# Mixture of experts behind a recurrent layer: four gathers that add themselves onto a tile, in place of four gathers and four additions

## The chip, the cores and the metric

The kernel runs on one core of one Trainium2 chip. It has TensorE (PE; its weight loads are shown as PEld), VectorE (DVE), ScalarE (ACT), GpSimd (POOL), SyncE (SP), which here only issues DMAs, and 16 DMA engines. The metric is the device time of one execution in microseconds (us); lower is better.

## The reference, cut to what matters

Eight sequences of 512 tokens, 512 wide, go through a layer norm. One branch is a linear attention with decay, gated and normed per head, and projected (s). The other is a mixture of 16 experts of which each token takes four, and a shared expert. The output is x + s * silu(mixture).

```python
routing_weights, selected_experts = jax.lax.top_k(router_probs, K)        # K = 4 of E = 16
routing_weights = routing_weights / routing_weights.sum(axis=-1, keepdims=True)
comb = jnp.sum(jax.nn.one_hot(selected_experts, E) * routing_weights[..., None], axis=1)
for e in range(E):
    mixed = mixed + comb[:, e:e + 1] * _swiglu(flat, Wg[e], Wu[e], Wd[e])
shared = _swiglu(flat, sWg, sWu, sWd)
g = silu(mixed + shared * sigmoid(flat @ shared_gate_w))
...
x = x + s * g
```

All is in float32. A tile is 128 tokens x 512; there are 32.

## The kernel before

**Stages.** First the norms, the routing and the shared expert of all sequences are worked out, beside the attention of sequence 0; the shared part of each tile, already times its gate, goes to DRAM (`sh_d`). The tokens' choices are sorted by expert into blocks of 128 rows. Then, after sequence 1, the blocks go through their experts; each row comes out times its routing weight and goes to DRAM (`y_d`). `place` holds, for each token and each of its four choices, the row of `y_d` that is its own. The last stage is the one that the change touches: the attention of sequences 2 to 7 on PE, and beside it, for all 32 tiles, the mixture and the final x + s * g.

**The mixture of one tile** is a generator, `mixture(b, t)` (L1190), that does one step at each call and yields between:

- step 1: SP loads the shared part from `sh_d` into the tile `m` (L1194, 12 buffers), and for the eight tiles of sequences 0 and 1 the stored projection `s` (L1198); POOL issues the first gather, an indirect DMA of 128 rows of `y_d` into a tile `yg` of its own (L1203, 14 buffers)
- steps 2 to 4: the other three gathers, each into its own `yg`
- step 5: POOL adds the second gather onto the first (L1209); step 6: POOL adds the fourth onto the third (L1212), and DVE adds the first sum onto `m` (L1214)
- step 7: DVE adds the second sum onto `m` (L1217)
- step 8: ACT takes the silu of `m` in place (L1220)
- step 9: for an `s` tile `last` is called; for the others `m` is kept until PE has projected the tile

`last` (L1227) loads x into `xo`, has DVE multiply `m` by `s` or by the projection `pw` in its PSUM bank (L1240), and POOL add it onto `xo` (L1244); SP stores the result (L1245). That last addition is put off by two steps (`late`), except in sequence 7.

**What sets the order.** Each engine has one queue and takes its instructions in order. `behind(engine)` puts an instruction behind the last one traced on that engine. `advance` (L1261) is one step for all open tiles; a new tile is opened each 11/5 steps. The attention's code calls it some 15 times per sequence between its parts, and its own instructions stand in the same queues: the products with the decays, the rotations (`stream_shuffle` L634, L636 to L638), the masked scores (L711) on DVE; the copies of `v` (L587), the silus of q and k (L632), the squares (L744) and the blocks of the state (L694) on ACT. PE multiplies for k and q (L627), v (L583), scores (L685), outputs (L722, L733), the sums of squares (L747) and the projections (L776, in two banks, and L906 in the last sequence).

Of the kernel before, what the change touches and what calls it, by code (L numbers as in the profile page):

```python
# [10 lines left out]
F32 = mybir.dt.float32  # L11
# [5 lines left out]
ALU = mybir.AluOpType  # L17
AX = mybir.AxisListType

P = 128  # L20
B, N, D = 8, 512, 512
# [74 lines left out]
def tile_block(ctx: ExitStack, tc: tile.TileContext, a: dict, out: bass.AP):  # L96
    nc = tc.nc
# [16 lines left out]
    y_d = dram.tile([NB * P, D], F32, name="y_d", tag="y_d")  # L114
# [96 lines left out]
    def behind(engine):  # L211

        last = next(
            (i for i in reversed(nc.cur_bb.bb.instructions) if i.engine == engine), None)
        return tc.issue_after(last) if last else nullcontext()

    POOL, DVE, ACT = (
        mybir.EngineType.Pool, mybir.EngineType.DVE, mybir.EngineType.Activation)
# [948 lines left out]
    with tc.If(count > SURE):  # L1167
# [16 lines left out]
    comb = right.enter_context(  # L1184
        tc.tile_pool(name="comb", bufs=1, side="right", reuse_waits="tile"))

    place = comb.tile([P, TOPK, NT], I32, tag="place", name="place")
    nc.sync.dma_start(place.rearrange("p r t -> p (r t)"), at_d)

    def mixture(b, t):  # L1190

        g = b * NC + t
        m = comb.tile([P, D], F32, tag="m", name=f"m_{b}_{t}", bufs=12)
        nc.sync.dma_start(m, sh_d[b][t * P : (t + 1) * P, :])  # L1194
        s = None
        if b < FIRST:
            s = comb.tile([P, D], F32, tag="s", name=f"s_{b}_{t}", bufs=4)
            nc.sync.dma_start(s, s_d[b][t * P : (t + 1) * P, :])  # L1198
        ys = []
        for r in range(TOPK):  # L1200
            yg = comb.tile([P, D], F32, tag="yg", name=f"yg_{b}_{t}_{r}", bufs=14)
            with behind(POOL):
                nc.gpsimd.indirect_dma_start(  # L1203
                    out=yg, out_offset=None, in_=y_d,
                    in_offset=bass.IndirectOffsetOnAxis(ap=place[:, r, g : g + 1], axis=0))
            ys.append(yg)
            yield
        with behind(POOL):
            nc.gpsimd.tensor_tensor(ys[0], ys[0], ys[1], ALU.add)  # L1209
        yield  # L1210
        with behind(POOL):
            nc.gpsimd.tensor_tensor(ys[2], ys[2], ys[3], ALU.add)  # L1212
        with behind(DVE):
            nc.vector.tensor_tensor(m, m, ys[0], ALU.add)  # L1214
        yield
        with behind(DVE):
            nc.vector.tensor_tensor(m, m, ys[2], ALU.add)  # L1217
        yield
        with behind(ACT):
            nc.scalar.activation(m, m, AF.Silu)  # L1220
        yield
        if s is not None:
            last(b, t, m, s)
        else:
            m_of[b, t] = m

    def last(b, t, m, s):  # L1227
        xo = comb.tile([P, D], F32, tag="xo", name=f"xo_{b}_{t}", bufs=4)
        nc.sync.dma_start(xo, x[b, t * P : (t + 1) * P, :])
        if (b, t) == (B - 1, NC - 1):  # L1230

            for cols in (slice(0, D // 2), slice(D // 2, D)):
                with behind(DVE):
                    nc.vector.tensor_tensor(m[:, cols], m[:, cols], s[:, cols], ALU.mult)
                with behind(DVE):
                    nc.vector.tensor_tensor(xo[:, cols], xo[:, cols], m[:, cols], ALU.add)
                nc.sync.dma_start(out[b, t * P : (t + 1) * P, cols], xo[:, cols])
            return
        with behind(DVE):
            nc.vector.tensor_tensor(m, m, s, ALU.mult)  # L1240

        def add():
            with behind(POOL):
                nc.gpsimd.tensor_tensor(xo, xo, m, ALU.add)  # L1244
            nc.sync.dma_start(out[b, t * P : (t + 1) * P, :], xo)  # L1245

        if b + 1 == B:
            add()
        else:
            late.append((steps[0], add))  # L1250
# [10 lines left out]
    def advance():  # L1261

        if steps[1] < len(tiles) and steps[0] * 5 >= steps[1] * 11:
            active.append(mixture(*tiles[steps[1]]))
            steps[1] += 1
        steps[0] += 1
        while late and late[0][0] + 1 < steps[0]:
            late.pop(0)[1]()
        order = active[:]
        while order:  # L1270
            f = order.pop(0)
            if next(f, f) is f:
                active.remove(f)
            order.reverse()
# [76 lines left out]
```

## Time and profile before

| | us |
|---|---|
| time, median of 3 runs | 1198.29 (1196.13 to 1202.39) |
| the profiled execution's own time | 1193.77 |
| its span in the profile | 1191.9 |
| first gather of the mixture starts | 742.1 |
| POOL: 128 gathers (L1203) busy | 143.0 |
| POOL: one addition of two gathered tiles (L1209), median | 1.284 |
| DVE: one addition onto `m` (L1214, L1217), median | 0.684 |

A row of the page's group list gives an engine, an instruction, what it writes and reads, how often, its busy time and the mean of one, and the idle time just ahead of it with what ended it. A row of the windows gives, for a stretch, its length and the busy time of PE, PEld, DVE, ACT and POOL, then the granted clock of TensorE and the share and rate of DMA. A row of the waits gives who waited for whom, the total, the number of times and the longest. A row of a timeline gives start, duration, engine and line; in square brackets is the idle time before it and what ended it. "issue" is time without a wait that the profile shows; an engine with q (SPq) is its queue.

### The profile page before, as it was taken

To read this page: it belongs to the slowest core of one execution; us is meant where nothing else is said; L and a number is where in the kernel's file an instruction comes from. 1 tells how busy PE (TensorE), PEld (TensorE's weight loads), DVE (VectorE), ACT (ScalarE), POOL (GpSimd) and SP (SyncE) were. 2 spreads that over 40 slices of the span, in tenths; PEclk is the share of its full clock that TensorE was granted. 3 is DMA by queue.
4 is the path that set the end of the run, shared out by engine and by line. 5 is a ranking of instruction groups with operands and counts; after the bars stand their busy time and mean duration, and the time that the engine had idled before them with its cause. 6 is when DMAs were issued, how large, how long until landed. Compare 5 with 4: busy or idle time off the path is not lost. (4 is left out here: it accounts for less than half of the span.)

```text
span 1191.9 us, 21613 instructions
## 1 busy us (share of the span) xinstructions
PE 1145.7 (96%) x7780; PEld 700.9 (59%) x7780; DVE 722.8 (61%) x1557; ACT 459.7 (39%) x934; POOL 452.2 (38%) x432
## 2 busy tenths in 40 slices
PE   7999999989999999999999999999999989999997
PEld 3445554456577777677777775555554645545553
DVE  6356754889124444344444444969979598698684
ACT  4444454144374444444444442251251422422531
POOL 3211203200213333233333331762886848858211
PEclk9998999989999999999999999999999999999999
DMA  9964341191659999899999895931845637534112
GB/s 340 327 236 173 120 168 44 41 377 38 183 160 224 226 227 221 217 232 232 221 227 229 229 226 181 336 120 51 277 133 184 200 95 235 163 115 144 36 35 73
DMA packets 163499, 217.42 MB, mean 182 GB/s; under 512 B 89536, under 2 KB 98880, under 8 KB 161472
## 3 DMA queue, kind: packets, MB, share of 16 engines
q1 hardware_dynamic: 141984, 144.10, 40.5%
q0 software_dynamic: 21120, 70.34, 21.4%
q8 instruction: 65, 1.06, 0.4%
q10 hardware_dynamic: 288, 1.57, 0.4%
q14 instruction: 42, 0.34, 0.1%
HBM read 125.71 MB, written 72.42 MB: 166 GB/s over the span
## 5 line engine op out<-in xcount | busy, mean ns | idle before, releaser
L1103 PE MATMUL pgu<-wexp,xt 128*128 x1088 | 257.8, 380 | 3.2 <-ACT xt L1084 2.7
L1103 PEld LDWEIGHTS pgu<-wexp,xt 128*128 128x128 f32 x1088 | 205.8, 190 | 90.9 <-issue 39.2
L1062 POOL DMA_INDIRECT xg<-xn_d,slot x79 | 75.1, 951 | 243.4 <-DVE y L1133 159.2
L1108 DVE TENSOR_TENSOR slb<-slb,pgu 128x128 f32<-128x128 f32 x136 | 39.2, 288 | 196.7 <-ACT slb L1107 142.0
L1203 POOL DMA_INDIRECT yg<-y_d,place x128 | 143.0, 1117 | 34.6 <-issue 18.6
L1086 ACT COPY xt<-pl 128x512 uint16<-128x512 uint16 x136 | 104.3, 767 | 134.1 <-DMA pl<-xg 77.5
L1124 PE MATMUL py<-wexp,hT 128*128 x272 | 139.3, 594 | 0.1
L583 PE MATMUL pv<-wv,xT 128*128 128x512 f32 x256 | 119.4, 602 | 3.5 <-ACT sh L372 2.3
L627 PE MATMUL pk<-xT,wk 128*128 128x512 f32 x256 | 118.2, 603 | 1.7 <-DVEq L1167 1.7
L627 PE MATMUL pq<-xT,wq 128*128 128x512 f32 x256 | 117.3, 599 | 0.0
L776 PE MATMUL pw<-wo,on 128*128 128x512 f32 x224 | 103.8, 612 | 5.8 <-DVE m L1240 5.2
L1244 POOL TENSOR_TENSOR xo<-xo,m 128x512 f32<-128x512 f32 x31 | 45.1, 1454 | 141.3 <-DVE m L1240 133.4
L1062 POOL DMA_INDIRECT more<-xn_d,slot x57 | 54.0, 947 | 109.9 <-DVE y L1133 109.0
L711 DVE TENSOR_TENSOR sc<-ps,dmask 128x512 f32<-128x512 f32 x128 | 79.5, 680 | 5.6 <-remote 3.8
L627 PEld LDWEIGHTS pq<-xT,wq 128*128 128x128 f32 x256 | 47.8, 193 | 52.8 <-issue 51.3
L627 PEld LDWEIGHTS pk<-xT,wk 128*128 128x128 f32 x256 | 46.1, 190 | 52.0 <-issue 49.6
L1133 DVE TENSOR_SCALAR y<-py,xg 128x512 f32<-128x512 f32 x79 | 59.3, 750 | 28.2 <-PE py L1124 27.7
L776 PEld LDWEIGHTS pw<-wo,on 128*128 128x128 f32 x224 | 42.5, 196 | 56.9 <-issue 47.8
L583 PEld LDWEIGHTS pv<-wv,xT 128*128 128x128 f32 x256 | 45.7, 191 | 49.6 <-issue 43.5
L1107 ACT ACTIVATE slb<-pgu 128x128 f32<-128x128 f32 x136 | 37.8, 278 | 87.5 <-PE pgu L1103 83.1
L694 ACT COPY blocked<-state 32x96 f32<-32x96 f32 x96 | 30.7, 320 | 81.6 <-DVE state L689 68.8
L1133 DVE TENSOR_SCALAR y<-py,more 128x512 f32<-128x512 f32 x57 | 42.7, 750 | 19.7 <-PE py L1124 19.6
(172 smaller groups left out, 1761.5 us busy)
## 6 DMA issues: line engine op xcount, KB each, us to landing
y_d<-y SPq DMA_DIRECT2D x136, 256.0 KB
wexp<-in_experts SPq DMA_DIRECT2D x14, 768.0 KB
sh_d<-sh SPq DMA_DIRECT2D x32, 256.0 KB
m<-sh_d SPq DMA_DIRECT2D x32, 256.0 KB
xo<-in_x SPq DMA_DIRECT2D x32, 256.0 KB
out<-xo SPq DMA_DIRECT2D x31, 256.0 KB
x<-in_x SPq DMA_DIRECT2D x7, 1024.0 KB
xT_d<-xT SPq DMA_DIRECT2D x7, 1024.0 KB
```

What stands on the lines that cost most here:

```text
L583: nc.tensor.matmul(pv, lhsT=xT_of[b][:, k, t * P : (t + 1) * P], rhs=wv[:, k, :], start=(k == 0), stop=(k == KC - 1))
L627: nc.tensor.matmul(ps, lhsT=w[:, k, g * P : (g + 1) * P], rhs=xT_of[b][:, k, :], start=(k == 0), stop=(k == KC - 1))
L711: nc.vector.tensor_tensor(s, pss[j].rearrange("p (c t) -> p c t", t=C), dmask[:, g * HG + j].unsqueeze(1).to_broadcast([P, NC, C]), ALU.mult)
L776: nc.tensor.matmul(pw, lhsT=on_of[b][:, g, t * P : (t + 1) * P], rhs=wo[:, g, :], start=(g == 0), stop=(g == G - 1))
L1062: nc.gpsimd.indirect_dma_start(out=row(i), out_offset=None, in_=xn_d, in_offset=bass.IndirectOffsetOnAxis(ap=slot[:, i : i + 1], axis=0))
L1086: nc.scalar.copy(xt[:, KP:, :].bitcast(U16).rearrange("p k (t h) -> p h k t", h=2), turned(i).rearrange("p (h k) t -> p h k t", h=2))
L1103: nc.tensor.matmul(pg[:, : 2 * F], lhsT=xt[:, k, :], rhs=wflat[:, bass.ds(off + k * 2 * F, 2 * F)], start=(k == 0), stop=(k == KC - 1))
L1108: nc.vector.tensor_tensor(sl, sl, pg[:, F : 2 * F], ALU.mult)
L1124: nc.tensor.matmul(py, lhsT=hT_of.pop(i), rhs=wflat[:, bass.ds(off_of.pop(i) + KC * 2 * F, D)], start=True, stop=True)
L1133: gone.append(nc.vector.tensor_scalar(y, py, row(i).bitcast(F32)[:, bass.ds(at, 1)], None, ALU.mult).ins)
L1203: nc.gpsimd.indirect_dma_start(out=yg, out_offset=None, in_=y_d, in_offset=bass.IndirectOffsetOnAxis(ap=place[:, r, g : g + 1], axis=0))
L1244: nc.gpsimd.tensor_tensor(xo, xo, m, ALU.add)
```

## The change

The four gathers of a tile no longer go to tiles of their own. Each has `compute_op=ALU.add` and `m` as its destination, so that the DMA reads the rows, adds them to what stands in `m` and writes the sums back. The four additions per tile on POOL and DVE are gone, and with them the tiles `yg`. A yield stands between the load of `m` and the first gather, and the steps of the additions are gone, so that a tile now takes seven steps: the load, four gathers, the silu, and the end. As all four gathers of a tile write the same `m`, each waits for the one before to land, and the first for the load of `m`.

```diff
@@ def mixture(b, t) @@
         if b < FIRST:
             s = comb.tile([P, D], F32, tag="s", name=f"s_{b}_{t}", bufs=4)
             nc.sync.dma_start(s, s_d[b][t * P : (t + 1) * P, :])
-        ys = []
+        yield
         for r in range(TOPK):
-            yg = comb.tile([P, D], F32, tag="yg", name=f"yg_{b}_{t}_{r}", bufs=14)
             with behind(POOL):
                 nc.gpsimd.indirect_dma_start(
-                    out=yg, out_offset=None, in_=y_d,
-                    in_offset=bass.IndirectOffsetOnAxis(ap=place[:, r, g : g + 1], axis=0))
-            ys.append(yg)
+                    out=m, out_offset=None, in_=y_d,
+                    in_offset=bass.IndirectOffsetOnAxis(ap=place[:, r, g : g + 1], axis=0),
+                    compute_op=ALU.add)
             yield
-        with behind(POOL):
-            nc.gpsimd.tensor_tensor(ys[0], ys[0], ys[1], ALU.add)
-        yield
-        with behind(POOL):
-            nc.gpsimd.tensor_tensor(ys[2], ys[2], ys[3], ALU.add)
-        with behind(DVE):
-            nc.vector.tensor_tensor(m, m, ys[0], ALU.add)
-        yield
-        with behind(DVE):
-            nc.vector.tensor_tensor(m, m, ys[2], ALU.add)
-        yield
         with behind(ACT):
             nc.scalar.activation(m, m, AF.Silu)
         yield
```

The lines below it move up by twelve: the gather is L1202 in the changed kernel, the silu L1208, the product of `last` L1228, the addition onto `xo` L1232.

## The prediction

> **What bounds the kernel now.** I read the page first (busy shares, slices), then the stage that the change touches by windows, then who waits for whom in it, then the timelines of DVE, PE, POOL and ACT around the two places where PE stands idle.
>
> The mixture runs from the first gather of expert rows at 742.1 us to the end, 449.9 us of the span. TensorE sets the time there as elsewhere:
>
> ```profile
> PE 1145.7 (96%) x7780; PEld 700.9 (59%) x7780; DVE 722.8 (61%) x1557; ACT 459.7 (39%) x934; POOL 452.2 (38%) x432
> 955.00:983.00 28.00, 24.72 (x144) 11.84 (x143) 25.70 (x44) 7.19 (x13) 12.12 (x12) 0.99 0.29 91
> 1036.00:1063.00 27.00, 24.83 (x144) 11.87 (x143) 24.60 (x43) 7.17 (x13) 12.64 (x12) 1.00 0.39 124
> 1120.00:1150.00 30.00, 30.00 (x238) 15.74 (x240) 28.46 (x57) 10.84 (x20) 0.00 (x0) 1.00 0.00 1
> sum 449.00, PE 433.13 PEld 235.60 DVE 352.04 ACT 140.17 POOL 270.36; mean PE 25.48 PEld 13.86 DVE 20.71 ACT 8.25 POOL 15.90
> ```
>
> Columns after the window: its length, then busy us of PE, PEld, DVE, ACT and POOL. PE is idle for 449.0 - 433.1 = 15.9 us of the stage; 5.0 of it lies after 1150, where no mixture runs. So no change to the mixture can win much over 11 us. The two windows with most idle PE, 3.3 and 2.2 us, are ones where DVE is nearly full. From 1120 on DVE is as full and PE loses nothing, so its share alone says little. The first of the two in detail:
>
> ```profile
> 958.43 2.14 DVE L637 TENSOR_TENSOR swk<-swk,sin 128x512 f32<-128x512 f32 x1
> 969.22 0.68 DVE L1214 TENSOR_TENSOR m<-m,yg 128x512 f32<-128x512 f32 x1
> 974.29 0.68 DVE L1217 TENSOR_TENSOR m<-m,yg 128x512 f32<-128x512 f32 x1
> 977.29 1.79 DVE L1214 TENSOR_TENSOR m<-m,yg 128x512 f32<-128x512 f32 x1
> 982.01 0.68 DVE L1240 TENSOR_TENSOR m<-m,pw 128x512 f32<-128x512 f32 x1
> 958.75 1.27 POOL L1209 TENSOR_TENSOR yg<-yg,yg 128x512 f32<-128x512 f32 x1
> 982.74 5.37 PE L776 MATMUL pw<-wo,on 128*128 128x512 f32 x8 [2.90 <-DVE m L1240]
> ```
>
> PE waits at 982.74 for DVE's multiply at 982.01, which frees the bank. DVE has no pause ahead of it from 957.2, and among what it did are the additions that go. L637 took 2.14 us where it takes 0.68 elsewhere: POOL's addition ran beside it. The eight matmuls after the gap took 5.37 us, not 3.6; the granted clock of the window from 983 to 1010 is 0.94.
>
> The other side of the account is POOL's queue and ACT's:
>
> ```profile
> L1203 POOL DMA_INDIRECT yg<-y_d,place x128: 945/1107/1467, 742.1 to 1107.3; - x128
> L1220 ACT ACTIVATE m<-m x32: 621/630/636, 781.4 to 1133.0; 128x512 f32<-128x512 f32 x32
> POOL xo L1244 <- DVE m L1240: 133.4, 18, 38.2
> ACT m L1220 <- DVE m L1217: 20.4, 13, 4.5
> 766.29 1.28 POOL L1212 TENSOR_TENSOR yg<-yg,yg 128x512 f32<-128x512 f32 x1 [1.40 <-DMA yg<-y_d,place]
> ```
>
> A gather keeps POOL 1.107 us. Today POOL never has to wait for one gather before the next, and only five times does it wait for a landing at all: it runs ahead until an xo addition (L1244) holds it for PE's projection. The silus (L1220) stand in ACT's queue between instructions that PE needs.
>
> **The change, part by part.** *Removed from DVE:* 64 additions of 0.60 us start to start, 38 us, and with them the stretching by POOL's additions. In the chain above: 0.6 + 0.6 + 1.7 of additions, 1.5 (L637) and 0.75 (L636 at 961.85, 1.43 us) of stretching, together 5.1 us, more than the 2.9 us that PE waits. So this gap would close, with the slow clock behind it (5.37 - 3.6 = 1.8). With the 2.2 us at 1062 that is 3.3 + 2.2 + 1.8 = 7 us; all idle time would be 11. Where DVE is not late, its additions lie beside matmuls and give nothing.
>
> *Removed from POOL:* 64 additions of 1.28 us, 82 us; no engine waits on POOL's busy time, so this gives only room.
>
> *Moved:* a tile takes seven steps, not nine. Its load of m (SP) now stands one step ahead of its first gather, and the gather waits for it; SP's loads and stores keep their number and order. This load is 256 KB and issued a step (about 5 us) ahead, so I cost it at nothing; where SP sits behind a store that waits for POOL's own xo addition, the price would be one landing, 2 to 3 us, beside the other tiles' gathers. The silu comes two steps earlier in ACT's queue: the last stands behind the ACT instruction that ended at 1126.2. ACT's function loads keep their order. The products of the eight s tiles (L1240) also come two steps earlier on DVE.
>
> *Added:* each gather after a tile's first must wait until the one before it has landed, since both write m. The program makes POOL wait, in order. Behind the waiting gather stand the other tiles' gathers and the xo additions; behind these, SP's stores and loads. Who waits for it is ACT at the silu, and behind the silu in ACT's queue stand the copies and silus of PE's banks (L587, L632) and the squares (L744) that PE multiplies at L747. This wait takes the place of those on DVE and POOL.
>
> *What one round costs.* The trace's semaphore updates, gather by gather, put the landing 2.57 us after the end of the issue at the median (2.0 at least; 3.0 at the upper quartile after 775 us; about 5, at most 6.6, while the stage's first loads run: the POOL line at 766.29 waited for a gather issued at 758.67 to 759.69). A round without any cost of adding is 1.11 + 2.57 + 0.15 to restart = 3.8 us. The Trainium skill (DMA: Bandwidth & Descriptors, Anatomy of one DMA) gives 2.0 us plus bytes over 436 GB/s, 2.6 us for 256 KB; by it the walk below would fit easily and the change would win its 7 us. The rows, 3.7 us before anything is added, decide. No row of the trace shows an accumulating DMA. Below: an addition could cost nothing, 3.8 us. Above: the skill (Collectives: The Full Stack, Why ReduceScatter is half of AllGather) has an adding DMA read two sources with two read descriptors per chunk, and the addition itself for free. A gather is 64 packets of 4 KB at 0.159 us over 16 engines, 0.64 us; a second read makes the landing 3.2. I bound the issue by twice today's, 2.2, and the landing by 5.3, what a busy DMA makes of it today. I take an estimated issue of 1.4 (a third more descriptor work for three descriptors instead of two would be 1.5) and a landing of 3.8 (3.2, and the 0.6 that a quarter of the landings exceed the median by today): a round of 5.3 us.
>
> *The walk down POOL's queue.* In the changed program's order, of 96 follow-on gathers 24 stand directly behind the one that they wait for, 54 have one other gather between, 18 two. Walking down it (a gather starts when POOL is free and its predecessor has landed, 0.25 us after each issue, 1.6 per xo addition, 24 of them) gives to the last landing: 291 us at 1.11/2.57, 324 at 1.11/3.2, 387 at 1.4/3.8, 464 at 2.2/3.8, 477 at 1.4/5.3. There are 384 us, from 742 to the last silu at 1126. On top come the holds for PE's projections: 68 us before 1126, of which the first (27.8) only uses up POOL's lead and the others (40) recur each sequence; and about 12 us for the slow landings at the start. At 1.4/3.8 that is 387 + 40 + 12 = 439, 55 over. If POOL, being late, meets none of the holds and none of the slow landings, 3 are over. Lateness swallows a hold only when POOL is already late, and then ACT waits already; I take about 60% of 55, +33 us. I count no relief of DVE in this case, since ACT then sets where PE waits.
>
> **The rivals.** *Faster: DVE's relief decides.* For it: the line at 982.74 and DVE's 25.70 of 28 us ahead of it. Against it: it needs a round of at most about 4 us (291 + 52 = 343, under 384 with a margin for local crowding); that is, adding must be nearly free. Then 1193.8 - 7 = 1187 in the profiled execution. Place: PE's gaps at 982 and 1062. *No change:* a round near 4.4 us (324 + 52 = 376), where small waits of ACT cost what DVE gains. *Much slower: POOL's chain is the bound.* At 2.2/3.8 or 1.4/5.3 the walk is 80 to 93 us over without any hold, 132 to 145 with all: +80 to +145. Against it: nothing but the lack of a reason for so dear an addition. DMA bandwidth is no bound: the engines are 46% busy in the stage, a second read adds 128 x 0.64 us, 82 of 450 us.
>
> **How the numbers follow.** The profiled execution took 1193.77 us, 4.5 below the median of the runs shown, 1198.29; changes are added to the median. Chances: a round near 5.3 us, +6 to +60, 0.53, at 1198.3 + 33 = 1231; much slower, 1278 to 1343, 0.22; no change, 1198, 0.15; faster, 1191, 0.10. A run of this kernel can tell about 0.5%, 6 us, from no change. The range leaves out the faster case and the dearest end: 1193 to 1315; the likeliest case alone spans 1204 to 1258.
>
> **What would show it.** Right: L1208's silus wait for the gathers by tens of us in sum, PE waits for ACT (L747, L627), DVE's stretched instructions get rarer and the wait at pw for m is gone; POOL's idle time stands before its gathers, its holds at xo shrink. Wrong: the silus wait no more than 20 us and the span falls by 7 (rounds under 4 us), or the issue itself grows past 2 us and POOL never waits for PE at all.

## The result, and the profile after

The changed kernel takes 1270.37 us (median; 1267.84 to 1271.67) against 1197.21 us for the kernel before, run beside it: a ratio of 1.0616, 95% interval 1.0588 to 1.0644, or 73 us more. The profiled span grew from 1191.9 to 1267.6 us, by 75.7.

First the page's line of busy time, then the stage from the start of the mixture by windows (after the length: busy us of PE, PEld, DVE, ACT and POOL, the granted clock, the DMA share), both of the changed kernel:

```profile
PE 1162.4 (92%) x7780; PEld 709.0 (56%) x7780; DVE 652.9 (52%) x1493; ACT 457.8 (36%) x934; POOL 427.2 (34%) x368
742.00:900.00 158.00, 135.24 (x1184) 75.19 (x1183) 87.94 (x155) 39.52 (x82) 77.29 (x50) 0.95 0.74 159
900.00:1050.00 150.00, 133.96 (x1029) 71.59 (x1029) 86.89 (x152) 41.86 (x79) 86.71 (x56) 0.93 0.75 150
1050.00:1191.00 141.00, 109.67 (x951) 60.77 (x952) 55.56 (x99) 39.54 (x76) 72.42 (x47) 0.88 0.65 112
sum 449.00, PE 378.86 PEld 207.55 DVE 230.40 ACT 120.92 POOL 236.42; mean PE 126.29 PEld 69.18 DVE 76.80 ACT 40.31 POOL 78.81
```

DVE is 69.9 us lighter and POOL 25.0, as the change intends. But PE, busy for 433 of these 449 us before, is now busy for 379. Of the 75.7 us of span, 59.0 are idle time of PE (1267.6 - 1162.4 = 105.2, against 46.2) and 16.7 are busy time: the same 7780 matmuls last longer, at a granted clock of 0.88 to 0.95 in these three windows, where before it was 0.99 to 1.00.

Who waits for whom, in the changed kernel (total us, times, longest), the first two lines from the whole span, the others from PE's waits between 742 and 1200 us:

```profile
ACT m L1208 <- DMA m<-y_d,place: 153.1, 23, 12.3
POOL m L1202 <- DMA m<-y_d,place: 152.3, 58, 6.2
PE pr L747 <- ACT on L617: 53.4, 5, 18.5
PE po L722 <- ACT blocked L694: 9.5, 3, 6.2
PE ps L685 <- ACT g L602: 4.2, 2, 3.6
PE pw L776 <- DVE m L1228: 1.9, 1, 1.9
```

The waits form a chain. POOL waits for a landing before the next gather of the same tile; ACT waits at the silu for the last landing; PE waits for ACT: 53.4 + 9.5 + 4.2 = 67.1 us. Before, no wait of PE in this stretch was put down to ACT, and all its waits there together made 11. The two together account for the idle time: 67 more of the one kind, some 9 less of the others. The wait for `m` at the projection's bank, which the prediction started from, is down to 1.9 us.

One such place in the timeline of the changed kernel, POOL, ACT and PE (start, duration; in brackets the idle time before it and what ended it):

```profile
890.72 1.54 POOL L1202 DMA_INDIRECT m<-y_d,place  x1 [1.28 <-DMA m<-y_d,place]
893.06 1.54 POOL L1202 DMA_INDIRECT m<-y_d,place  x1 [0.80 <-DMA m<-y_d,place]
...
898.04 0.63 ACT L1208 ACTIVATE m<-m 128x512 f32<-128x512 f32 x1 [10.20 <-DMA m<-y_d,place]
898.57 2.17 ACT L744 ACTIVATE sq<-on 128x512 f32<-128x512 f32 x4
900.76 1.28 ACT L617 ACT_TABLE_LOAD   x1
902.05 2.06 ACT L617 ACTIVATE on<-p 128x512 f32<-128x512 f32 x4
...
891.71 3.70 PE L583 MATMUL pv<-wv,xT 128*128 128x512 f32 x8
902.71 1.94 PE L747 MATMUL pr<-sq,sel 128*32 128x128 f32 x32 [7.29 <-ACT on L617]
904.57 5.14 PE L627 MATMUL pk<-xT,wk 128*128 128x512 f32 x8
```

ACT stands at the silu for 10.20 us until the tile's last gather has landed. Directly behind that silu in its queue are the squares (L744) and the gate (L617) that PE's next product needs, so PE stands for 7.29 us. The eight matmuls of L627 after it take 5.14 us where they take 3.7 at the full clock; in the window over them the granted clock is 0.66. So this stop of PE is paid for a second time.

```profile
902.00:910.00 8.00, 7.29 (x42) 3.83 (x43) 0.95 (x1) 6.34 (x11) 5.22 (x4) 0.66 0.71 101
```

The gathers and silus themselves, after (min/median/max in ns), and the DMA queue of the gathers, of after in the first fence and of before in the second (packets, MB, share of 16 engines):

```profile
L1202 POOL DMA_INDIRECT m<-y_d,place x128: 1530/1548/2066, 748.1 to 1185.8; - x128
L1208 ACT ACTIVATE m<-m x32: 622/629/631, 773.4 to 1202.3; 128x512 f32<-128x512 f32 x32
q0 software_dynamic: 29312, 70.34, 29.7%
```

```profile
q0 software_dynamic: 21120, 70.34, 21.4%
```

An adding gather keeps POOL 1.60 us in the mean, not 1.117. From the trace's semaphore updates it lands 3.70 us after the end of its issue at the median and 3.98 in the mean (before 2.57; 2.86 in the mean after 775 us). It is recorded as 128 packets of 2 KB at 0.178 us (median), not 64 of 4 KB at 0.159. The first gather starts at 748.13 instead of 742.08, and the last silu at 1202.3 instead of 1133.0, 69 us later.

### The profile page after: what moved, and what is told of

It reads as the page before. It is cut to its first block, busy times and chain, and to the rows that moved or that the text cites. A ratio compares the mean times of both kernels' runs of the same rounds, so it can differ in the third digit from the quotient of the medians.

```text
span 1267.6 us, 21491 instructions
## 1 busy us (share of the span) xinstructions
PE 1162.4 (92%) x7780; PEld 709.0 (56%) x7780; DVE 652.9 (52%) x1493; ACT 457.8 (36%) x934; POOL 427.2 (34%) x368
## 3 DMA queue, kind: packets, MB, share of 16 engines
q0 software_dynamic: 29312, 70.34, 29.7%
## 5 line engine op out<-in xcount | busy, mean ns | idle before, releaser
L1202 POOL DMA_INDIRECT m<-y_d,place x128 | 204.4, 1597 | 195.2 <-DMA m<-y_d,place 152.3
L627 PE MATMUL pk<-xT,wk 128*128 128x512 f32 x256 | 126.1, 637 | 1.7 <-DVEq L1167 1.7
L583 PE MATMUL pv<-wv,xT 128*128 128x512 f32 x256 | 122.0, 613 | 3.4 <-ACT sh L372 2.3
L627 PE MATMUL pq<-xT,wq 128*128 128x512 f32 x256 | 117.1, 598 | 0.0
L627 PEld LDWEIGHTS pk<-xT,wk 128*128 128x128 f32 x256 | 49.3, 203 | 57.6 <-issue 55.2
L1232 POOL TENSOR_TENSOR xo<-xo,m 128x512 f32<-128x512 f32 x31 | 48.8, 1595 | 86.6 <-issue 56.8
L627 PEld LDWEIGHTS pq<-xT,wq 128*128 128x128 f32 x256 | 47.8, 193 | 52.8 <-issue 52.7
L1208 ACT ACTIVATE m<-m 128x512 f32<-128x512 f32 x32 | 20.1, 629 | 153.2 <-DMA m<-y_d,place 153.1
L1133 DVE TENSOR_SCALAR y<-py,xg 128x512 f32<-128x512 f32 x79 | 59.2, 749 | 26.8 <-PE py L1124 26.4
L747 PE MATMUL pr<-sq,sel 128*32 128x128 f32 x224 | 12.5, 380 | 53.8 <-ACT on L617 53.4
```

The source lines that it names most:

```text
L583: nc.tensor.matmul(pv, lhsT=xT_of[b][:, k, t * P : (t + 1) * P], rhs=wv[:, k, :], start=(k == 0), stop=(k == KC - 1))
L627: nc.tensor.matmul(ps, lhsT=w[:, k, g * P : (g + 1) * P], rhs=xT_of[b][:, k, :], start=(k == 0), stop=(k == KC - 1))
L1133: gone.append(nc.vector.tensor_scalar(y, py, row(i).bitcast(F32)[:, bass.ds(at, 1)], None, ALU.mult).ins)
L1202: nc.gpsimd.indirect_dma_start(out=m, out_offset=None, in_=y_d, in_offset=bass.IndirectOffsetOnAxis(ap=place[:, r, g : g + 1], axis=0), co ...
```

## The experiments

All ratios are to the kernel before, run on the same chip in the same batch (medians 1196.9, 1185.5 and 1197.7 us in the three batches); the times that were expected start from about 1197. "Step" is one call of a tile's generator. A diff shows the lines that matter; "..." marks what is left out.

**The chain without adding.** The same chain of four, in the same places, but each gather is a plain one, so that nothing is summed.

```diff
-                    compute_op=ALU.add)
+                    )
```

> The changed kernel with plain gathers: compute_op is left out, so the four gathers of a tile overwrite m one after another, each still waiting for the one before; nothing is summed. Same order, same waits, cheaper rounds (issue 1.1, landing about 2.6 to 2.9 us instead of 1.6 and 4.0). Theory (POOL's chain of rounds; the silus in ACT's queue pass its lateness to PE): a round near 4 us fits between the silus, so ACT waits for gathers fall from 153 us to under 20 and the time is within 10 us of before, 1190 to 1207. Rival 1 (any wait in POOL's in-order queue holds xo additions and stores, whatever a round costs): still 1230 or more. Rival 2 (the adding transfer itself, chained or not): as the theory; it is told apart by add_no_chain.

1192.36 us, 0.9963 (0.9941 to 0.9986). Issue 0.99 us and landing 3.01 in the mean, 2.70 at the median. Waits of this run:

```profile
POOL m L1202 <- DMA m<-y_d,place: 114.3, 53, 6.0
ACT m L1207 <- DMA m<-y_d,place: 23.5, 10, 8.1
PE pr L747 <- ACT on L617: 8.3, 2, 6.6
```

So the serial chain and the earlier place of the silu cost little when the round is cheap: what they cost is at most what the missing additions gain, which the runs below put at 0.8% to 1.4%. (ACT's waits, 23.5 us, are a little over the 20 expected.) POOL waits 114 us for landings here too, and it does little harm. In this order of the gathers, a round of 0.99 + 3.01 + 0.15 = 4.15 us is short enough; one of 1.60 + 3.98 + 0.15 = 5.7 is not.

**Adding without the chain.** The first gather of a tile adds onto `m`, the other three onto twelve sink tiles in turn, zeroed once, so that hardly a gather waits for another. Three parts of each sum are left out of the result.

```diff
+    sinks = [comb.tile([P, D], F32, tag=f"sink{j}", name=f"sink{j}") for j in range(12)]
...
-                    out=m, out_offset=None,
+                    out=sinks[(g * 3 + r - 1) % 12] if r else m, out_offset=None,
```

> The changed kernel with the same 128 adding gathers, but three of a tile's four add onto twelve tiles of their own in turn (set to zero once), so that no gather waits for one of its own tile; these three parts of the sum are left out of the output. Issue and landing should stay near 1.6 and 4.0 us. Theory (the chain is what costs): ACT's waits for gathers vanish and the time falls to before less DVE's relief, 1185 to 1200. Rival 2 (the dearer issue and the transfers of 2 KB packets cost by themselves, through POOL's busy time or the DMA engines): still 1230 or more.

1180.87 us, 0.9861 (0.9825 to 0.9897), a little under the range expected. The issue is as dear as in the changed kernel (1.55 us at the median, 128 gathers), and POOL waits 0.6 us in all for gathers. The dear issue alone, the small packets and the added DMA traffic therefore cost nothing that shows; it needs the chain.

**No additions at all.** The kernel before without the four additions; the gathers go to their own tiles.

```diff
-            nc.gpsimd.tensor_tensor(ys[0], ys[0], ys[1], ALU.add)
...
-            nc.gpsimd.tensor_tensor(ys[2], ys[2], ys[3], ALU.add)
-            nc.vector.tensor_tensor(m, m, ys[0], ALU.add)
...
-            nc.vector.tensor_tensor(m, m, ys[2], ALU.add)
```

> The kernel before with its four additions per tile left out, three yields in their place: the gathers go to their own tiles and nobody reads them. It shows what freeing DVE and POOL of the additions is worth by itself. Forecast of the prediction: PE's gaps near 982 and 1062 close, 7 us faster, about 1190, at most 11. If the additions lay wholly beside matmuls: 1197, no change.

1260.97 us, 1.0523 (1.0487 to 1.0558): a miss. It was meant to measure what the additions cost, and it is nearly as slow as the changed kernel, though no gather waits for another. A stretch of its windows, and of its timelines of POOL and PE:

```profile
742.00:760.00 18.00, 13.03 (x79) 6.88 (x77) 8.16 (x18) 2.34 (x5) 13.86 (x14) 0.87 1.03 389
760.00:800.00 40.00, 29.93 (x233) 15.15 (x233) 20.82 (x41) 5.38 (x15) 13.06 (x14) 0.72 0.51 179
762.28 0.95 POOL L1203 DMA_INDIRECT yg<-y_d,place  x1 [0.30 <-issue]
763.54 0.95 POOL L1203 DMA_INDIRECT yg<-y_d,place  x1 [0.30 <-issue]
764.79 0.94 POOL L1203 DMA_INDIRECT yg<-y_d,place  x1 [0.31 <-issue]
761.12 1.01 PE L627 MATMUL pk<-xT,wk 128*128 128x512 f32 x1 [1.05 <-issue]
763.22 1.01 PE L627 MATMUL pk<-xT,wk 128*128 128x512 f32 x1 [1.09 <-issue]
```

With nothing to hold it, POOL issues gather after gather (28 of them up to 776 us), and PE stands for about 1.05 us between single matmuls without a wait that the profile shows. It comes back with each such row: PE is full from 800 to 850 us, where POOL issues two gathers, and not from 850 to 900, where it issues 20 in a row from 872 us on.

```profile
800.00:850.00 50.00, 50.00 (x414) 26.95 (x413) 28.90 (x54) 20.22 (x37) 3.18 (x3) 1.00 0.05 16
850.00:900.00 50.00, 35.96 (x309) 19.64 (x308) 20.30 (x35) 6.19 (x14) 32.34 (x31) 0.85 0.79 259
```

The next run tells whether the rows are the cause.

**The same, with POOL's queue held.** The kernel before, but VectorE's two additions left out, and POOL's two done on a scratch tile (`pace`), so that the experts' rows are left out of the result.

```diff
-            nc.gpsimd.tensor_tensor(ys[0], ys[0], ys[1], ALU.add)
+            nc.gpsimd.tensor_tensor(pace, pace, pace, ALU.add)
...
-            nc.gpsimd.tensor_tensor(ys[2], ys[2], ys[3], ALU.add)
-            nc.vector.tensor_tensor(m, m, ys[0], ALU.add)
+            nc.gpsimd.tensor_tensor(pace, pace, pace, ALU.add)
...
-            nc.vector.tensor_tensor(m, m, ys[2], ALU.add)
```

> The kernel before without VectorE's two adds of the expert rows, and with GpSimd's two adds working on a scratch tile that no gather fills, so they keep their place and length and wait for nothing; the rows of the experts are left out of the result. It differs from the run without any of the four adds in that GpSimd's queue is held again between gathers. Theory (that run's 1261 us came of gathers issued back to back, beside which TensorE stood idle for about 1 us at a time with nothing to wait for): 1180 to 1192 us. Rival (the loss there came of the tiles that nobody reads, or of VectorE's adds being away): about 1260 us again.

1176.45 us, 0.9919 (0.9893 to 0.9946). Its first window:

```profile
742.00:760.00 18.00, 18.00 (x100) 8.78 (x99) 16.11 (x27) 4.10 (x9) 12.96 (x13) 1.00 0.98 362
```

At nearly the same DMA share (0.98 against 1.03) PE is full. So the loss of the run before came of the unbroken rows of gathers, not of VectorE's missing additions or the unread tiles. What starves PE there is not shown. And VectorE's additions, with POOL's no longer waiting for rows, are worth 0.8%, about 9 us (6 to 13 by the interval), when nothing else is late.

**Where the silu stands.** The changed kernel with empty steps between the last gather and the silu: two (which gives ACT the very order that it had before), three and six. The steps move a second thing, which the expectations did not have in view. `advance` takes the open tiles from the two ends of its list in turn, and a tile that waits for its silu stays in the list, so the tiles' gathers interleave differently in POOL's queue. Of the 96 gathers that must wait for one before them, 24 stand directly behind it in the changed kernel, 18 with two steps, 7 with three and 7 with six (counted in the program's order).

```diff
+        for _ in range(6):
+            yield
         with behind(ACT):
             nc.scalar.activation(m, m, AF.Silu)
```

Six steps, twice (the second time with more executions):

> The changed kernel with six more yields ahead of the silu, which puts it some six steps (about 30 us) later in ACT's queue; gathers, chain and all else stay. Theory (PE is held only through ACT, which stands at a silu whose gathers have not landed; POOL has the time if nobody asks early): ACT's waits fall below 20 us and the time comes to 1188 to 1208. Rival 3 (POOL's chain is the throughput bound of the stage: its rounds need some 440 us from the first gather on, and the xo additions behind them hold stores, loads and projections): 1235 or more, with the waits moved from the silus to DVE's products.

> The run with six empty steps ahead of the silu once more, in more rounds and beside the other two, to rank the three. Every theory expects 0.985 to 0.992 of the kernel before, as the first time (0.988); the question is only whether it stands apart from the two chains with a later add.

1183.06 us, 0.9881 (0.9821 to 0.9942), under the range expected, and 1189.59 us, 0.9930 (0.9902 to 0.9957), just over it.

Two steps, and three:

> The changed kernel with two steps put between a tile's last gather and its silu, so that ACT's order is the one of the kernel before; the adding chain of four stays. Theory (the loss is made where a silu stands in ACT's queue before its rows have landed): two steps are some 6 us of a walk of 3.0 us a gather, and the 23 waits of the silus, 6.7 us each in the changed kernel, mostly go; about 1205 us (1190 to 1225), with 20 to 60 us of ACT waits on the gathers left instead of 153. Rival (the chain on POOL is too slow in sum, whatever ACT's order): 1250 us or more.

> The changed kernel with three empty steps between a tile's last gather and its silu; nothing of the chain is changed. Theory (each step of ACT's lead takes a share of the silus' lateness away until none is late: 0 steps 73 us over the kernel before, 2 steps 46, 6 steps 14 under): between the last two on a straight line, 2% to 3% over the kernel before, with some 50 us of silu waits left. Rival (a threshold: once a silu is later than one chain nothing waits any more): within 0.5% of the run with six steps, a ratio of 0.988.

1228.01 us, 1.0393 (1.0329 to 1.0457) with two steps: between theory and rival, so neither had it right. 1202.37 us, 1.0032 (1.0007 to 1.0058) with three: under the straight line and over the threshold. Between two and three steps the order of the gathers changes most (18 to 7 directly behind). The first waits are of the run with two steps, the second of the one with three:

```profile
POOL m L1202 <- DMA m<-y_d,place: 149.9, 66, 6.9
ACT m L1210 <- DMA m<-y_d,place: 83.0, 18, 16.0
PE pr L747 <- ACT on L617: 35.7, 4, 14.5
PE po L722 <- ACT blocked L694: 5.3, 2, 3.7
```

```profile
POOL m L1202 <- DMA m<-y_d,place: 120.4, 65, 6.7
ACT m L1210 <- DMA m<-y_d,place: 13.5, 3, 7.8
PE pr L747 <- ACT on L617: 9.9, 3, 6.7
```

And the run with six steps, first time: POOL still waits 127.4 us, and nobody behind it does.

```profile
POOL m L1202 <- DMA m<-y_d,place: 127.4, 67, 7.7
ACT m L1210 <- DMA m<-y_d,place: 1.1, 1, 1.1
sum 384.00, PE 381.56 PEld 211.14 DVE 251.67 ACT 129.01 POOL 236.17; mean PE 381.56 PEld 211.14 DVE 251.67 ACT 129.01 POOL 236.17
```

The last line is the window from the first gather (744.8) to the issue of the last (1128.8). PE is full, and the walk takes 384.0 us. In the changed kernel, from 748.1 to 1185.8, it takes 437.7, POOL's busy time being the same:

```profile
sum 437.70, PE 367.56 PEld 202.56 DVE 224.91 ACT 117.90 POOL 234.87; mean PE 367.56 PEld 202.56 DVE 224.91 ACT 117.90 POOL 234.87
```

The same 128 gathers and 24 additions onto `xo` stand in these two windows. With two steps the walk is 406.6 us, with three 381.8. Most of this is the order. The third and the fourth gather of one tile, in the changed kernel, where nothing stands between them, and with six steps, where another tile's gather (806.17) does:

```profile
806.59 1.54 POOL L1202 DMA_INDIRECT m<-y_d,place  x1 [2.11 <-DMA m<-y_d,place]
812.21 1.54 POOL L1202 DMA_INDIRECT m<-y_d,place  x1 [4.08 <-DMA m<-y_d,place]
```

```profile
802.18 1.54 POOL L1202 DMA_INDIRECT m<-y_d,place  x1 [0.30 <-issue]
806.17 1.54 POOL L1202 DMA_INDIRECT m<-y_d,place  x1 [2.44 <-DMA m<-y_d,place]
808.01 1.82 POOL L1202 DMA_INDIRECT m<-y_d,place  x1 [0.30 <-issue]
```

Ahead of the gathers that stand directly behind their predecessor POOL is idle for 93.0 us in the changed kernel, for 76.7 with two steps, 32.2 with three and 33.5 with six. Walked down with each trace's own issues and landings and with nothing else to wait for, the four orders take 415, 402, 379 and 382 us, by an estimate from the traces. So some 33 of the 54 us are the order. The rest is about what POOL waits at `xo`: 17.3 + 2.6 us in the changed kernel's walk, none with six steps. The longest of these waits, 6.04 us, ended at 1121.95, right behind a product of DVE on a projection (L1228, 1121.13, 0.68 us): there the stopped PE may well come back to POOL, but no run shows that apart.

Three and six steps have the same count of 7 and nearly the same walk, and differ in the silu: with it three steps later, PE's 9.9 us of waiting for ACT are gone and the ratio falls by 1.0% to 1.5%. Between the changed kernel and three steps both things move, and how the time divides between them is not shown: no run has the one without the other. That the chain's pace is no bound is not shown either, since the later silu came with a shorter walk.

**The chain loosened.** One empty step after each gather, so that other tiles' gathers stand in between, and the same with three more steps ahead of the silu:

```diff
                     compute_op=ALU.add)
             yield
+            yield
...
+        for _ in range(3):
+            yield
         with behind(ACT):
             nc.scalar.activation(m, m, AF.Silu)
```

> The changed kernel with an empty step after each of a tile's four gathers, so that other tiles' gathers stand between two gathers of one tile, and the silu comes four steps later than in the changed kernel. Theory (a round of 5.6 us is spent waiting because the next gather of the same tile comes too soon): POOL's waits on the gathers fall from 152 us to under 60, the last gather issues before 1110 us, and the time is 1175 to 1190 us. Rival (issue at 1.6 us and the DMA share set POOL's pace, not the landings): the last gather stays near 1129 us, as with the later silu, and the time is not under 1183 us.

> The empty step after each gather and three more ahead of the silu. Theory (with the steps between gathers alone, POOL still waited 61 us on landings and ACT 9 us, and the time was 0.997; three steps more take ACT's 9 us and the 6 us of TensorE behind it): a ratio of 0.985 to 0.992. Rival (the spread chain's cost is in a tile's whole residence, 14 steps, against 12 buffers of the tile m, so a later silu makes the next tile's load late): 0.997 or more.

1181.70 us, 0.9971 (0.9947 to 0.9994) and 1177.16 us, 0.9834 (0.9803 to 0.9866). POOL's waits on landings are 60.8 and 42.5 us, the silus' 9.2 and none; 8 and 2 gathers stand directly behind their predecessor. In the first, the waits stayed just over 60 us and the last gather issued at 1113 us, not before 1110 as expected. The second has the lowest ratio of the study, 1.7% under the kernel before, a little better than expected; its interval overlaps with those of the two next best.

**Two chains of two.** Two gathers add onto `m`; the other two go to a tile of their own, one plain and one adding, in turns with the first two; VectorE adds that tile onto `m`. Then the same with two steps ahead of that addition.

```diff
-        for r in range(TOPK):
+        y = comb.tile([P, D], F32, tag="yg", name=f"yg_{b}_{t}", bufs=6)
+        for r in (1, 0, 3, 2):
...
-                    out=m, out_offset=None, in_=y_d,
+                    out=m if r % 2 == 0 else y, out_offset=None, in_=y_d,
...
-                    compute_op=ALU.add)
+                    **({} if r == 1 else {"compute_op": ALU.add}))
             yield
+        yield          # the second run alone
+        yield          # the second run alone
+        with behind(DVE):
+            nc.vector.tensor_tensor(m, m, y, ALU.add)
+        yield
```

> Two adding chains of two gathers in place of one of four: two experts' rows go to a tile of their own (one plain gather, one adding), two are added onto the shared part, the chains alternate in POOL's queue, and VectorE adds the two tiles once (one step more before the silu). Theory (it is the serial chain of four that is late): a wait only where the gather between is shorter than the landing, so about half of the 152 us of POOL waits go, silus wait under 30 us, time 1180 to 1195 us. Rival (the price is in the slower issue and the smaller packets, 128 of 2 KB for each gather): 1230 us or more.

> The two adding chains with two empty steps ahead of VectorE's add, so that neither the add nor the silu comes before the rows have landed. Theory (what is left over in the two chains is VectorE's 20 us and ACT's 19 us of waiting for them, some of which reaches TensorE): a ratio of 0.985 to 0.990 to the kernel before, against 0.993 without the steps. Rival (TensorE was full, so those waits cost nothing): 0.993 again.

1177.57 us, 0.9929 (0.9903 to 0.9954) and 1183.37 us, 0.9877 (0.9843 to 0.9911); the two intervals overlap a little, so that the two steps bring something is likely, not shown. POOL's waits on landings fall to 26.4 and 16.9 us over both tiles, by more than the half that was expected. The silus wait for no DMA, but 19.1 and 11.2 us for DVE's addition; in the first run that addition waited 19.7 us for landings itself.

**The runs with gathers that add or stand in a chain, on one scale.** What goes with the time is how long PE waits for ACT between 742 and 1200 us, more than how long POOL waits for landings. The second column counts the gathers directly behind the one that they wait for. The kernel with six steps gave 0.9881 and 0.9930, so rows closer than half a per cent are not ranked.

| kernel | directly behind | ratio to before | ACT at the silus, us | PE for ACT, us | POOL for landings, us |
|---|---|---|---|---|---|
| changed | 24 | 1.0616 | 153.1 | 67.1 | 152.3 |
| silu two steps later | 18 | 1.0393 | 83.0 | 41.0 | 149.9 |
| silu three steps later | 7 | 1.0032 | 13.5 | 9.9 | 120.4 |
| step after each gather | 8 | 0.9971 | 9.2 | 5.9 | 60.8 |
| chain without adding | 24 | 0.9963 | 23.5 | 8.5 | 114.3 |
| silu six steps later (second) | 7 | 0.9930 | none | none | 127.5 |
| two chains | 0 | 0.9929 | 19.1, for DVE | 2.9 | 26.4 |
| silu six steps later (first) | 7 | 0.9881 | 1.1 | none | 127.4 |
| two chains, later addition | 0 | 0.9877 | 11.2, for DVE | none | 16.9 |
| adding without the chain | - | 0.9861 | none | none | 0.6 |
| step after each gather, silu later | 2 | 0.9834 | none | none | 42.5 |

## Why the prediction was right in its mechanism and too small in its size

**Direction, mechanism and signs: right.** The silus wait for the gathers by tens of us in sum, PE waits for ACT at L747 (and at L722 and L685; not at L627, which the prediction named beside it), POOL's idle time stands before its gathers, and its waits at `xo` for DVE's product fell from 133.4 to 29.8 us (56.8 more there are put down to "issue"). DVE's stretched multiplications at L637 are gone (the longest is 0.71 us, before 2.15); at L636 they are not (3.05, before 2.15), and one of POOL's additions onto `xo` runs beside each long one. The rivals "faster" and "no change" named their conditions, a round of at most about 4 us and one near 4.4: the chain without adding has 4.15 us and stands between them, 0.4% under the kernel before. That no engine waits on POOL's busy time was not quite so: before, DVE waited 4.9 us for POOL's additions (L1214, L1217).

**The issue of 1.4 us and the landing of 3.8: a little low.** Measured means: 1.60 and 3.98; the round is 5.7 us, not 5.3. The bounds 1.11 to 2.2 and 2.57 to 5.3 held both. Three descriptors in place of two, as the prediction counted them, would be half more work, not a third: 1.66 us as an estimate, near the 1.60 measured; no run shows the descriptors. The trace's own row of 2.57 us plus a second read would have been worse. The Trainium skill's 2.0 us plus bytes over 436 GB/s (DMA: Bandwidth & Descriptors, Anatomy of one DMA) gives 2.6 us for what measures 1.55 + 3.70 us here at the median. And its account of an addition in the DMA, free but for a second read (Collectives: The Full Stack, Why ReduceScatter is half of AllGather), gives no figure for what the runs show: 0.48 us more issue (means) and 1.13 us more landing (medians). The records hold the same bytes in twice the packets; a second read is not visible as such. By the shares of the gathers' queue (29.7% and 21.4% of the spans) the packets take about 121 us more of the 16 engines, not 82; that this is no bound, as the prediction said, the run without the chain bears out.

**The walk of 439 us: near the measured figure, by luck.** From the first gather to the last landing (748.1 to 1190.8 us, by the semaphore updates) it took 443 us. But two errors cancel. The rounds were too cheap: with the measured 1.60 and 3.98 the same walk comes to 416 us, not 387. And the holds were too dear: 19.9 us of waits at `xo` stand in the walk, where 40 were added, with 12 for slow landings.

**"About 60% of 55": this is the step that failed.** It rested on the sum just named: without the holds only 3 us were to be over, so lateness would swallow most of the 55. With the measured round the rounds alone are 416 - 384 = 32 us over, and no lateness swallows those. In the prediction's own terms the overrun was 65 us (last landing at 1190.8, last place of the silu at 1126), and the span grew by 75.7: more than all of it, not 60%. What comes on top has its place in the trace. Behind its stops PE was clocked lower (0.66 in the window shown): 16.7 us of busy time, a cost that the prediction counted where a gap closes (1.8 us) and put at nothing where gaps open. Nor is the loss one lag at the end: ACT is held 23 times, 6.7 us in the mean, and 67.1 of its 153.1 us reach PE, in each sequence anew (at L747 7.15, 7.29, 8.52, 18.50 and 11.90 us).

**The load of `m` costed at nothing: not nothing.** The first gather waited for it (POOL 12.2 us), and started 6 us later (748.13 against 742.08); 2.6 of these are a later start of PE's work there too. That start is much the same in the run with six steps (744.8 to 748.4), which is faster than the kernel before; so with the silus later it costs little. Its share in the changed kernel was not tried by itself.

**DVE's relief, 7 us where nothing is late: somewhat low.** Without VectorE's additions, 9 us; with all of them gone and no chain, 16; with the late silu, 8 to 14. The bound of 11 us of idle time left out that a PE with fewer gaps also spends less busy time: in the run with six steps PE's idle time is 36.3 us (before 46.2) and its busy time 1141.8 (before 1145.7). In the changed kernel the relief does not show beside the lateness.

**Open.** How the 73 us divide between the order of the gathers and the place of the silu is not shown; a run with the changed kernel's order and a later silu, or with the order of the three steps and the early silu, would tell. How much of the time is due to the round's dearer issue (0.61 us more than the plain chain's) and how much to its landing (0.97) was not separated either.

## What to carry to other kernels

When work moves from an engine into a chain of dependent DMAs, the chain's total against the time at hand is not enough. Write down the order in which the links stand in the issuing queue, for a link directly behind its predecessor waits nearly a whole landing (93.0 us over 24 links here); and find the in-order queue in which the consumer of the last link stands, and what stands behind it. Here the same gathers and additions cost 73 us, or won 8 to 14, by empty steps alone, which put other tiles' gathers between the links and the consumer later. So cost the change with the links of several chains interleaved and with a later consumer; with both, the addition in the DMA was worth 1.7%.

## What the runs showed of the hardware that was not expected

- An indirect DMA that adds holds POOL 1.55 us at the median where a plain one holds it 0.95 to 1.1, and lands 3.70 us after the end of its issue where the plain one lands after 2.57; it shows as 2 KB packets of 0.178 us in place of 4 KB packets of 0.159.
- Plain gathers issued one straight after another, every 1.25 us and 28 in a row, left PE idle for about 1 us at a time with no wait in the profile, and cost 5.2%; the same gathers with additions between them on POOL did not, at a DMA share of 0.98 against 1.03. A lighter POOL queue made the kernel slower; why is not shown.
- After a stop PE ran slower: the eight matmuls behind the 7.29 us stop took 5.14 us instead of 3.7, at a granted clock of 0.66, and the windows of the stage had 0.88 to 0.95.
